# Twenty gathered and twenty-nine multiplied blocks in the first layer of a four-layer graph network, with one-hots of 784 columns

## The chip, the cores and the metric

The kernel runs on one core of one Trainium2 chip. The metric is the time of one execution in microseconds of device time. Three runs of the kernel before took 2024.36, 2024.81 and 2026.46 us; the median is 2024.81 us.

## What is computed

6250 nodes with 256 features each, 100,000 directed edges sorted by destination. The input is normalised and cut at zero, then four layers follow. Each adds to every node the rows of its neighbours (`segment_sum`) and sends the sum through three matrices. Cut to what matters:

```python
def agg(h):
    return jax.ops.segment_sum(h[src], dst, num_segments=N)

for l in range(NL - 1):                     # three layers
    h = x + agg(x)
    h = relu(h @ W1s[l] + b1s[l])
    h = relu(h @ W2s[l] + b2s[l])
    x = h @ W3s[l] + b3s[l]
h = x + agg(x)                              # the head
h = relu(h @ cW1 + cb1)
h = relu(h @ cW2 + cb2)
return h @ cW3 + cb3

h = maximum(layernorm(x), 0.0)
x = x + gnn(h, src, dst, ...)
```

## The kernel before

**Blocks.** The nodes form 49 blocks of 128. The first 24 blocks are re-sorted by degree; they are called "s", and block 0 has the nodes with fewest edges. The other 25 are called "u" and keep their order. The first matrix of a layer is multiplied in ahead of the sum over neighbours, so what a layer adds up is `XY`: for each of the 49 source blocks a high and a low part of 256 columns, kept on chip.

**Two ways to add up.** The sum for a destination block is made in one of two ways.

- *Multiplied.* A block of the adjacency matrix, 49 x 128 x 128 counts of one byte, is built once, stored (`mats`), fetched in each layer (`at<-mat`, line 1279), cast to a number type of the matmul (`a<-at`, lines 1896 to 1901, on ScalarE and VectorE) and multiplied with `XY` on TensorE (line 1928). Destination blocks are taken together in *panels* of up to four. A panel goes through 49 *units*, one for each source block, and a unit has four matmuls of 128 columns for each destination block of the panel.
- *Gathered.* For each node of a degree-sorted block its neighbours' rows are fetched by indirect DMAs that GpSimd issues (`rows<-table`, line 1613), one DMA for each rank of neighbour, and added two at a time: the first pair is copied on ScalarE (line 1645), the others are added on VectorE (lines 1649 and 1651). The sum `u` (lines 1666 and 1667) is transposed on TensorE (`pt`, line 1676).

The lists in `sorted_edges` divide the blocks. `seq` names the 32 blocks that are built, in the order of building; `early`, `wide` and `final` cut them into the panels of layer 0, of layers 1 and 2 and of the head, in places of `seq`; `nodes_of` names the gathered groups of each layer. Before, layer 0 multiplies 30 blocks in panels of 3, 4, 4, 4, 4, 4, 4 and 3, and gathers 19.

**Building.** While layer 0 runs, `build` makes the adjacency blocks, 8 *batches* of 4 one-hot pairs for each block (257 batches in all). A batch is a one-hot `lo` of 4 x 128 columns (line 1197), a one-hot `hi` of 4 x 98 columns times a weight (line 1215, one instruction for each of the four), four matmuls of 98 columns (line 1245) and an eviction to bytes (`at<-bp`, line 1253, every eighth on VectorE at line 1255). The values that are compared with come from small copies on ScalarE (`pairs`, `marks`, lines 1190 and 1192).

**The order of work.** The instruction stream of each engine is fixed when the program is made. `build` and `listed` are generators: one yield of `build` is a batch. `listed` makes the list of the neighbours of the degree-sorted blocks: six groups of three VectorE operations (lines 1702, 1706 and 1711), then the edge lists fetched by GpSimd (`lane<-padded`, line 1734), then six groups that turn them into row numbers (`some`, `idxN`, lines 1752 to 1757), then the rows of the high s blocks for the builder. First comes a stage of `PRE` batches, in which nothing is multiplied yet: 8 for each block of the first panel, and 4 more. Then the panels run, and `goals` spreads the remaining batches over their units, so that a panel's blocks are ready when it begins. In each unit `listed` is taken on by one yield.

The gathers are spread over a layer by a planned clock (`work_of`, `pace`), and each waits for the matmul that was the last one in the program when it was issued, so GpSimd can't run ahead of TensorE by more than planned. `XY` has to be replaced between layers. The MLP of each panel and each gathered group (`second`, line 1408; `third`, lines 1505 and 1510) is put into the units of later panels; its rows go to the next table, s blocks through one indirect DMA each (`place_rows`, lines 594 and 596, a *place*), also on GpSimd, in between the gathers. The last panel of a layer, and the last gathered block, are done in a hurry ahead of the next layer.

Of the kernel before, what the change touches and what calls it, by code (L numbers as in the profile page):

```python
# [9 lines left out]
F32 = mybir.dt.float32  # L10
# [410 lines left out]
def sorted_edges(  # L421
# [39 lines left out]
    nc = tc.nc  # L461
    N, C = x.shape
    (E,) = src.shape
    NLAYER = W1s.shape[0]
# [3 lines left out]
    NT = -(-N // P)  # L468
# [3 lines left out]
    GSUB = 64 // GD  # L472
    TWO = GD // 2
    HW = NT * TWO
# [4 lines left out]
    BATCH = 4  # L479
# [52 lines left out]
    clT = const.tile([P, 3, GSUB, 2 * BUILT], BF16, name="clT")  # L532
# [10 lines left out]
    cT, weigh, loT = clT[:, 0], clT[:, 1], clT[:, 2]  # L543
# [553 lines left out]
    with tc.manual_schedule():  # L1097
# [77 lines left out]

        pairs, marks = {}, {}

        def pair(hots, k):

            if k < len(batches):  # L1180
                slot, s, half, q0 = batches[k]
                if s is None:
                    pairs[slot, 2] = hots.tile([P, BATCH, 2], BF16, name="more", bufs=1)
                    nc.vector.tensor_copy(pairs[slot, 2],
                                          extra[:, 2, :, None].to_broadcast([P, BATCH, 2]))
                    marks[slot, 2] = hots.tile([P, 2, BATCH], F32, name="moremarks", bufs=1)
                    nc.vector.tensor_copy(marks[slot, 2], extra[:, :2])
                elif q0 == 0:
                    pairs[slot, half] = hots.tile([P, GSUB, 2], BF16, name="pairs", bufs=3)
                    nc.scalar.copy(pairs[slot, half], loT[:, :, s, None].to_broadcast([P, GSUB, 2]))  # L1190
# [3 lines left out]
        def one_hot(o, values, which, n):  # L1194

            shape = [P, BATCH, n // 2, 2]
            nc.vector.tensor_tensor(  # L1197
                o.rearrange("p q (n t) -> p q n t", t=2),
                values.rearrange("p (n t) -> p n t", t=2)[:, None, :, :].to_broadcast(shape),
                which[:, :, None, :].to_broadcast(shape), OP.is_equal)  # L1200

        def low_hot(hots, k):
            if k < len(batches):
                slot, s, half, q0 = batches[k]
                lo = hots.tile([P, BATCH, P], BF16, name="lo", bufs=2)
                one_hot(lo, lanes, pairs[slot, 2] if s is None else pairs[slot, half][:, q0:q0 + BATCH], P)
                hot[k] = [lo]

        def high_hot(hots, k):
            if k < len(batches):  # L1210
                slot, s, half, q0 = batches[k]
                hi = hots.tile([P, BATCH, HW], BF16, name="hi", bufs=2)
                w, o = (marks[slot, 2], 0) if s is None else (marks[slot, half], q0)
                for q in range(BATCH):
                    nc.vector.tensor_scalar(hi[:, q, :], cols, w[:, 0, o + q:o + q + 1],  # L1215
                                            w[:, 1, o + q:o + q + 1], op0=OP.is_equal, op1=OP.mult)
                hot[k].append(hi)

        own_at = [None]

        def build(hots, ats, ps_b):


            each = GSUB // BATCH
            pair(hots, 0)
            low_hot(hots, 0)
            high_hot(hots, 0)
            step, held = 0, None
            for k, (slot, s, half, q0) in enumerate(batches):
# [13 lines left out]
                for m in range(BATCH):  # L1243
                    for i, (lo, hi) in enumerate(sets):
                        mm = nc.tensor.matmul(bp[:, m * HW:(m + 1) * HW], lo[:, m, :], hi[:, m, :],  # L1245
                                              start=(i == 0), stop=(i == len(sets) - 1))
# [16 lines left out]
                if s is None:  # L1263
                    held = None
                    low_hot(hots, k + 1)
                    high_hot(hots, k + 1)
                yield
# [429 lines left out]
        def listed(pool, ps_b):  # L1697
# [50 lines left out]
            for b0, n in nodes_of[0]:  # L1748
                r, o = wide_of[b0], starts_of[b0]
                shape = [P, n, r]  # L1750
                some = pool.tile(shape, F32, name="some", bufs=1)
                nc.vector.tensor_tensor(some, colf[:, None, :r].to_broadcast(shape),
# [313 lines left out]
```

## Time and profile before

| | |
|---|---|
| median of three runs | 2024.81 us |
| profiled execution, its own time | 2030.06 us |
| its span, first to last instruction | 2028.2 us |
| TensorE (PE) busy in the span | 1909.6 us, 94% |
| VectorE (DVE) busy | 1118.4 us, 55% |
| ScalarE (ACT) busy | 1080.1 us, 53% |
| GpSimd (POOL) busy | 1304.6 us, 64% |
| mean granted TensorE clock | 0.972 |
| DMA traffic | 361.47 MB, mean 178 GB/s |

The shares are means over stages that differ. The span has a preparation up to about 135 us, the stage of `PRE` batches up to 183.4 us, layer 0 up to 717.6 us, layers 1 and 2 up to 1594 us, and the head. Of the views of the profile, the one by windows gives each engine's busy time in each of these, and the timeline tells what a single instruction waited for. A duration in the timeline is that of the instruction; where one engine's instructions overlap, the distance from start to start tells its rate.

### The profile page before, as it was taken

To read this page: it belongs to the slowest core of one execution; us is meant where nothing else is said; L and a number is where in the kernel's file an instruction comes from. 1 tells how busy PE (TensorE), PEld (TensorE's weight loads), DVE (VectorE), ACT (ScalarE), POOL (GpSimd) and SP (SyncE) were. 2 spreads that over 40 slices of the span, in tenths; PEclk is the share of its full clock that TensorE was granted. 3 is DMA by queue.
4 is the path that set the end of the run, shared out by engine and by line. 5 is a ranking of instruction groups with operands and counts; after the bars stand their busy time and mean duration, and the time that the engine had idled before them with its cause. 6 is when DMAs were issued, how large, how long until landed. Compare 5 with 4: busy or idle time off the path is not lost. (4 is left out here: it accounts for less than half of the span.)

```text
span 2028.2 us, 29980 instructions
## 1 busy us (share of the span) xinstructions
PE 1909.6 (94%) x9236; PEld 1477.3 (73%) x9236; DVE 1118.4 (55%) x2984; ACT 1080.1 (53%) x2228; POOL 1304.6 (64%) x1444
## 2 busy tenths in 40 slices
PE   5856999999999899999999999999999999999997
PEld 3643667677777777777789777777789777777765
DVE  7779989898876634334344443333335344443433
ACT  4634667676676555444444564444445464454442
POOL 2525556666766637677777656776777466777775
PEclk9876999999999999999999999999999999999998
DMA  5513546666656746556556675555557576665553
GB/s 167 172 59 121 166 148 210 198 203 188 208 175 192 227 151 191 171 180 184 170 174 189 195 225 172 169 169 179 179 173 214 160 233 191 197 190 178 181 174 106
DMA packets 252342, 361.47 MB, mean 178 GB/s; under 512 B 33353, under 2 KB 206313, under 8 KB 252155
## 3 DMA queue, kind: packets, MB, share of 16 engines
q1 hardware_dynamic: 188160, 190.34, 29.7%
q0 software_dynamic: 61952, 166.87, 27.6%
q10 hardware_dynamic: 2058, 2.25, 0.4%
q8 instruction: 74, 1.21, 0.3%
q14 instruction: 98, 0.79, 0.1%
HBM read 292.33 MB, written 67.40 MB: 177 GB/s over the span
## 5 line engine op out<-in xcount | busy, mean ns | idle before, releaser
L1928 PE MATMUL agg<-a,XY 128*128 128x512 f32 (+1 forms) x6272 | 1510.7, 393 | 16.0 <-DVE a L1901 9.6
L1613 POOL DMA_INDIRECT rows<-table,idxN x1121 | 1084.0, 967 | 493.5 <-PE agg L1928 205.8
L1928 PEld LDWEIGHTS agg<-a,XY 128*128 128x128 f32 x6272 | 1144.3, 189 | 254.6 <-issue 15.0
L1899 ACT CAST a<-at 128x512 fp32r<-128x512 uint8 (+1 forms) x1249 | 707.4, 601 | 239.6 <-PE agg L1928 228.9
L1649 DVE TENSOR_TENSOR sums<-sums,rows 128x512 f32<-128x512 f32 x477 | 333.1, 698 | 483.9 <-DMA rows<-table,idxN 441.7
L1215 DVE TENSOR_SCALAR hi<-cols,marks 128x98 bf16<-128x98 bf16 x1024 | 250.7, 326 | 0.0
L1901 DVE CAST a<-at 128x512 fp32r<-128x512 uint8 (+1 forms) x312 | 141.2, 459 | 167.4 <-PE agg L1928 141.9
L1253 ACT CAST at<-bp 128x392 uint16<-128x392 f32 x227 | 111.0, 489 | 144.6 <-PE bp L1245 141.6
L1245 PE MATMUL bp<-hi,lo 128*128 128x98 bf16 x1028 | 118.7, 215 | 34.9 <-DVE hi L1215 31.5
L1245 PEld LDWEIGHTS <-lo 128*128 128x128 bf16 x1028 | 61.3, 100 | 111.1 <-DVE hi L1215 65.7
L1408 PE MATMUL ps<-h,w 128*128 128x512 f32 (+2 forms) x336 | 135.8, 548 | 0.0
L1505 PE MATMUL ps<-w,h 128*128 128x256 f32 x588 | 133.7, 379 | 0.0
L1197 DVE TENSOR_TENSOR lo<-lanes,pairs 128x512 bf16<-128x512 bf16 x256 | 107.0, 418 | 29.7 <-PE bp L1245 25.1
L1505 PEld LDWEIGHTS ps<-w,h 128*128 128x128 f32 x588 | 111.2, 190 | 15.8
L596 POOL DMA_INDIRECT table<-zz,ids x72 | 72.1, 1002 | 68.8 <-DVE zz L1510 48.4
L1645 ACT COPY sums<-rows 128x512 f32<-128x512 f32 x74 | 43.8, 592 | 123.8 <-DMA rows<-table,idxN 93.7
L1411 ACT ACTIVATE h<-ps,bias 128x512 f32<-128x512 f32 (+2 forms) x84 | 51.7, 636 | 96.0 <-PE ps L1408 95.8
L1510 DVE TENSOR_TENSOR zz<-ps,w 128x512 f32<-128x512 f32 (+1 forms) x81 | 50.4, 637 | 94.5 <-PE ps L1505 87.5
L1408 PEld LDWEIGHTS ps<-h,w 128*128 128x128 f32 x336 | 63.1, 193 | 52.4 <-issue 37.3
L1684 ACT ACTIVATE h<-pt,bias 128x256 f32<-128x256 f32 (+1 forms) x84 | 33.1, 446 | 126.6 <-PE pt L1676 125.3
L1335 DVE TENSOR_TENSOR XY<-back,XY 128x256 fp32r<-128x256 f32 x138 | 54.1, 421 | 42.5 <-ACT XY L1334 41.9
L1942 ACT ACTIVATE h<-agg,bias 128x512 f32<-128x512 f32 (+1 forms) x60 | 37.3, 670 | 73.5 <-PE agg L1928 73.3
(235 smaller groups left out, 889.3 us busy)
## 6 DMA issues: line engine op xcount, KB each, us to landing
at<-mat SPq DMA_DIRECT2D x140, 448.0 KB
mat<-at SPq DMA_DIRECT2D x32, 784.0 KB
at<-mat SPq DMA_DIRECT2D x62, 336.0 KB
rows<-table,idxN POOLq DMA_INDIRECT x1121
back<-table SPq DMA_DIRECT2D x138, 128.0 KB
table<-zz SPq DMA_DIRECT2D x35, 256.0 KB
at<-mat SPq DMA_DIRECT2D x63, 112.0 KB
own<-zz SPq DMA_DIRECT2D x55, 128.0 KB
```

What stands on the lines that cost most here:

```text
L596: got = nc.gpsimd.indirect_dma_start(out=ap, out_offset=bass.IndirectOffsetOnAxis(ap=ids[:, b:b + 1], axis=0), in_=sb, in_offset=None)
L1197: nc.vector.tensor_tensor(o.rearrange("p q (n t) -> p q n t", t=2), values.rearrange("p (n t) -> p n t", t=2)[:, None, :, :].to_broadcast( ...
L1215: nc.vector.tensor_scalar(hi[:, q, :], cols, w[:, 0, o + q:o + q + 1], w[:, 1, o + q:o + q + 1], op0=OP.is_equal, op1=OP.mult)
L1245: mm = nc.tensor.matmul(bp[:, m * HW:(m + 1) * HW], lo[:, m, :], hi[:, m, :], start=(i == 0), stop=(i == len(sets) - 1))
L1253: nc.scalar.copy(o, v)
L1408: mm = nc.tensor.matmul(ps[:, :w], weights[l][0][:, c, i * P:(i + 1) * P], h1[:, c, :w], start=(c == 0), stop=(c == KC - 1))
L1505: mm = nc.tensor.matmul(o, h2[0][:, c, nodes], w3[:, c, :], start=(c == 0), stop=(c == KC - 1))
L1613: got = nc.gpsimd.indirect_dma_start(out=t[:, c % 2, :], out_offset=None, in_=tables[self.l][:, :], in_offset=bass.IndirectOffsetOnAxis(ap ...
L1649: nc.vector.tensor_tensor(sums, sums, rows.rearrange("p h c -> p (h c)"), OP.add)
L1899: nc.scalar.copy(o, v)
L1901: nc.vector.tensor_copy(o, v)
L1928: mm = nc.tensor.matmul(agg[c][:, :w], XY[:, j, o:o + P], a[:, :w], start=(i == 0 and half == 0), stop=(i == NT - 1 and half == 1))
```

## The change

Layer 0 gathers 20 blocks instead of 19 and multiplies 29 instead of 30, in panels of 2, 3 and six of 4 blocks. `seq` still has 32 blocks, in another order; layers 1 and 2 still multiply 30 blocks, in panels of 4, 4, 4, 4, 3, 4, 4 and 3; the head's panels keep their sizes. `hi` is made for two batches at a time, by one comparison over 8 x 98 columns and one multiplication in place with the weights, and its values come from one copy on ScalarE instead of two.

```diff
-    seq = [("u", b) for b in range(NS, NT - 3)] + [("s", b) for b in range(NS - 1, NS - 6, -1)] + [
-        ("u", b) for b in range(NT - 3, NT)] + [("s", NS - 6), ("s", NS - 7)]
-    early = [(0, 3)] + [(b, 4) for b in range(3, 27, 4)] + [(27, 3)]
-    wide = [(b, 4) for b in range(0, 24, 4)] + [(24, 3), (27, 3)]
+    seq = [("u", b) for b in range(NS, NT - 6)] + [("s", b) for b in range(NS - 1, NS - 5, -1)] + [
+        ("u", b) for b in range(NT - 6, NT)] + [("s", b) for b in range(NS - 5, NS - 8, -1)]
+    early = [(0, 2), (2, 3)] + [(b, 4) for b in range(5, 29, 4)]
+    wide = [(b, 4) for b in range(0, 16, 4)] + [(16, 3), (19, 4), (26, 4), (23, 3)]
...
-    nodes_of = [[(15, 4), (11, 4), (7, 4), (4, 3), (1, 3), (0, 1)]] * NLAYER + [
+    nodes_of = [[(16, 4), (12, 4), (8, 4), (4, 4), (1, 3), (0, 1)]] + [
+        [(15, 4), (11, 4), (7, 4), (4, 3), (1, 3), (0, 1)]] * (NLAYER - 1) + [
         [(13, 4), (9, 4), (5, 4), (1, 4), (0, 1)]]
...
-                    pairs[slot, half] = hots.tile([P, GSUB, 2], BF16, name="pairs", bufs=3)
-                    nc.scalar.copy(pairs[slot, half], loT[:, :, s, None].to_broadcast([P, GSUB, 2]))
-                    marks[slot, half] = hots.tile([P, 2, GSUB], F32, name="marks", bufs=3)
-                    nc.scalar.copy(marks[slot, half], clT[:, :2, :, s])
+                    pairs[slot, half] = hots.tile([P, 3, GSUB, 2], BF16, name="pairs", bufs=3)
+                    nc.scalar.copy(pairs[slot, half],
+                                   clT[:, :, :, s, None].to_broadcast([P, 3, GSUB, 2]))
...
+        def compare(o, values, which, op):
+
+            n, width = o.shape[1], o.shape[2]
+            shape = [P, n, width // 2, 2]
+            o = o.rearrange("p q (n t) -> p q n t", t=2)
+            if values is None:
+                values = o
+            else:
+                values = values.rearrange("p (n t) -> p n t", t=2)[:, None, :, :].to_broadcast(shape)
+            nc.vector.tensor_tensor(o, values, which[:, :, None, :].to_broadcast(shape), op)
...
         def high_hot(hots, k):
             if k < len(batches):
-                slot, s, half, q0 = batches[k]
-                hi = hots.tile([P, BATCH, HW], BF16, name="hi", bufs=2)
-                w, o = (marks[slot, 2], 0) if s is None else (marks[slot, half], q0)
-                for q in range(BATCH):
-                    nc.vector.tensor_scalar(hi[:, q, :], cols, w[:, 0, o + q:o + q + 1],
-                                            w[:, 1, o + q:o + q + 1], op0=OP.is_equal, op1=OP.mult)
-                hot[k].append(hi)
+                codes, o, n = of(k)
+                hi = hots.tile([P, 2 * BATCH, HW], BF16, name="hi", bufs=2)
+                compare(hi[:, :n], cols, codes[:, 0, o:o + n], OP.is_equal)
+                compare(hi[:, :n], None, codes[:, 1, o:o + n], OP.mult)
+                for i in range(n // BATCH):
+                    hot[k + i] = [hi[:, i * BATCH:(i + 1) * BATCH]]
...
                 if s is not None:
                     low_hot(hots, k + 1)
-                    high_hot(hots, k + 1)
+                    if q0 % (2 * BATCH) == 0:
+                        high_hot(hots, k + 2)
...
-                some = pool.tile(shape, F32, name="some", bufs=1)
+                some = pool.tile(shape, F32, name="moved", bufs=2)
```

`lo` is made as before, by `compare` too (it now has line 1201, as the two instructions of `hi` have). The first panel has two blocks, so `PRE` is 8 x 2 + 4 = 20 batches instead of 28.

Three places show how the instructions move. The first is VectorE at the start of the stage of `PRE` batches; `hi` and `lo` are the one-hots, `cols` and `lanes` the column numbers they are compared with, `lane` the first piece of `listed`. Before:

```order
L1053 COPY zs<-bp 128x256
L1197 TENSOR_TENSOR lo<-lanes,pairs 128x512
L1215 TENSOR_SCALAR hi<-cols,marks 128x98 x4
L1197 TENSOR_TENSOR lo<-lanes,pairs 128x512
L1215 TENSOR_SCALAR hi<-cols,marks 128x98 x4
L1702 TENSOR_TENSOR lane<-lanes,goal 128x512
```

and now:

```order
L1054 COPY zs<-bp 128x256
L1201 TENSOR_TENSOR hi<-cols,pairs 128x784
L1201 TENSOR_TENSOR hi<-hi,pairs 128x784
L1201 TENSOR_TENSOR lo<-lanes,pairs 128x512 x2
L1201 TENSOR_TENSOR hi<-cols,pairs 128x784
L1201 TENSOR_TENSOR hi<-hi,pairs 128x784
L1712 TENSOR_TENSOR lane<-lanes,goal 128x512
```

Two batches take ten instructions before and four now, and `hi` stands two batches ahead of the matmuls that read it instead of one.

The second place is TensorE at the end of layer 0's last panel: `agg` are the products, four to a unit, `pt` the transposes of a gathered sum, and `ps` at line 1515 the third matrix of the gathered group of blocks 4 to 7. Before:

```order
L1928 MATMUL agg<-a,XY 128x384 x32
L1676 MATMUL pt<-ident,u 128x128 x2
L1928 MATMUL agg<-a,XY 128x384 x36
L1676 MATMUL pt<-ident,u 128x128 x2
L1408 MATMUL ps<-h_8787,w_1366 128x384 x4
L1928 MATMUL agg<-a,XY 128x384 x4
```

and now:

```order
L1938 MATMUL agg<-a,XY 128x512 x36
L1515 MATMUL ps<-w_1368,h_7852 128x256 x8
L1938 MATMUL agg<-a,XY 128x512 x24
L1686 MATMUL pt<-ident,u 128x128 x2
L1938 MATMUL agg<-a,XY 128x512 x8
L1686 MATMUL pt<-ident,u 128x128 x2
L1938 MATMUL agg<-a,XY 128x512 x4
```

The last row of transposes, at unit 48 of 49 in both, is that of the last gathered block; the third matrix of a gathered group now stands 8 units ahead of it.

The third is GpSimd over the same stretch; `rows` are gathers, `table` with `ids` are places. Before:

```order
L1613 DMA rows<-table_87,idxN 128x256 x5
L596 DMA table_88<-zz,ids 6378x256
L594 MEMSET mark 1x4
...
L596 DMA table_88<-zz,ids 6378x256
L1613 DMA rows<-table_87,idxN 128x256 x5
L1613 DMA rows<-table_87,ids 128x256
```

and now:

```order
L1623 DMA rows<-table_87,idxN 128x256 x9
L597 DMA table_88<-zz,ids 6378x256
L595 MEMSET mark 1x4
...
L597 DMA table_88<-zz,ids 6378x256
L1623 DMA rows<-table_87,idxN 128x256
L1623 DMA rows<-table_87,ids 128x256
```

Four places stand in each; six gathers follow them before, and two now. Over the whole layer the gathers are 330 instead of 309, and the places 20 in both.

More of the change, by code (lines that the diff above doesn't have):

```diff
@@ L1174, in sorted_edges @@
         hot = {}
-        pairs, marks = {}, {}
+        pairs = {}
         def pair(hots, k):
@@ L1194, in one_hot @@
[L1194 to L1200, printed above, removed]
+                    pairs[slot, 2] = hots.tile([P, 3, BATCH, 2], BF16, name="more", bufs=1)
+                    nc.vector.tensor_copy(pairs[slot, 2], extra[:, :, :, None].to_broadcast(
+                        [P, 3, BATCH, 2]))
+                elif q0 == 0:
+                    pairs[slot, half] = hots.tile([P, 3, GSUB, 2], BF16, name="pairs", bufs=3)
+                    nc.scalar.copy(pairs[slot, half],
+                                   clT[:, :, :, s, None].to_broadcast([P, 3, GSUB, 2]))
@@ new lines, in compare, with of @@
+        def compare(o, values, which, op):
[7 more added lines that the diff above has]
+            nc.vector.tensor_tensor(o, values, which[:, :, None, :].to_broadcast(shape), op)
+        def of(k):
+            slot, s, half, q0 = batches[k]
+            if s is None:
+                return pairs[slot, 2], 0, BATCH
+            assert q0 % (2 * BATCH) == 0
+            return pairs[slot, half], q0, 2 * BATCH
@@ L1205, in low_hot @@
                 lo = hots.tile([P, BATCH, P], BF16, name="lo", bufs=2)
[L1206 to L1207 removed]
+                codes, o = (pairs[slot, 2], 0) if s is None else (pairs[slot, half], q0)
+                compare(lo, lanes, codes[:, 2, o:o + BATCH], OP.is_equal)
+                hot[k].append(lo)
         def high_hot(hots, k):
             if k < len(batches):
[L1211 to L1217 removed]
+                codes, o, n = of(k)
[4 more added lines that the diff above has]
+                    hot[k + i] = [hi[:, i * BATCH:(i + 1) * BATCH]]
         own_at = [None]
@@ L1225, in build @@
             pair(hots, 0)
+            high_hot(hots, 0)
             low_hot(hots, 0)
-            high_hot(hots, 0)
             step, held = 0, None
@@ L1243, in build @@
                 for m in range(BATCH):
-                    for i, (lo, hi) in enumerate(sets):
+                    for i, (hi, lo) in enumerate(sets):
                         mm = nc.tensor.matmul(bp[:, m * HW:(m + 1) * HW], lo[:, m, :], hi[:, m, :],
@@ L1264, in build @@
                     held = None
+                    high_hot(hots, k + 1)
                     low_hot(hots, k + 1)
-                    high_hot(hots, k + 1)
                 yield
```

5 lines of the change are left out of this document (removed).

## The prediction

> **What bounds the kernel now.** I read the windows first, cut at the stages of the program: the stage of `PRE` batches, layer 0's first and second panel, its next five, the last but one and the last (the cuts lie within a microsecond of the panels' ends).
>
> ```profile
> core 0: us, PE busy (x) PEld busy (x) DVE busy (x) ACT busy (x) POOL busy (x), PEclk, DMA share, GB/s
> 131.00:183.40 52.40, 27.60 (x140) 12.49 (x139) 48.80 (x182) 18.25 (x52) 16.15 (x18) 0.55 0.26 83
> 183.40:251.00 67.60, 59.31 (x356) 45.62 (x356) 64.00 (x252) 40.11 (x105) 40.15 (x42) 0.92 0.51 158
> 251.00:321.00 70.00, 66.84 (x475) 46.61 (x476) 62.85 (x261) 46.47 (x102) 38.60 (x40) 1.00 0.54 170
> 321.00:585.00 264.00, 263.12 (x1460) 188.28 (x1459) 229.71 (x766) 187.86 (x409) 173.01 (x183) 1.00 0.63 197
> 653.00:718.90 65.90, 54.36 (x292) 46.06 (x293) 35.51 (x97) 38.31 (x97) 37.72 (x41) 0.92 0.58 182
> ```
>
> The first two rows belong to VectorE: 48.80 of 52.40 and 64.00 of 67.60 us busy, while TensorE idles or runs at a low granted clock. From 321 us TensorE is full, and 263.12 of 264.00 us leave only its own work to save. The last row has idle TensorE again. The timeline says what VectorE repeats in the first stage, one batch every 1.25 us:
>
> ```profile
> 135.28 0.42 DVE L1197 TENSOR_TENSOR lo<-lanes,pairs 128x512 bf16<-128x512 bf16 x1 [3.01 <-ACT pairs L1190]
> 137.68 0.68 DVE L1702 TENSOR_TENSOR lane<-lanes,goal 128x512 bf16<-128x512 bf16 x1
> 139.25 0.42 DVE L1197 TENSOR_TENSOR lo<-lanes,pairs 128x512 bf16<-128x512 bf16 x1
> 171.26 0.41 DVE L1197 TENSOR_TENSOR lo<-lanes,pairs 128x512 bf16<-128x512 bf16 x1
> 171.59 1.00 DVE L1215 TENSOR_SCALAR hi<-cols,marks 128x98 bf16<-128x98 bf16 x4
> 171.95 0.93 PE L1245 MATMUL bp<-hi,lo 128*128 128x98 bf16 x4 [0.32 <-DVE hi L1215]
> 172.51 0.41 DVE L1197 TENSOR_TENSOR lo<-lanes,pairs 128x512 bf16<-128x512 bf16 x1
> 183.41 1.62 PE L1928 MATMUL agg<-a,XY 128*128 128x384 f32 x4 [1.99 <-DVE a L1897]
> ```
>
> `lo` takes 0.33 us from start to start, the four `hi` 0.92, and the matmuls wait for `hi`. The last panel's idle time is one wait:
>
> ```profile
> 695.44 1.01 POOL L596 DMA_INDIRECT table<-zz,ids  x1 [0.30 <-issue]
> 696.75 0.99 POOL L596 DMA_INDIRECT table<-zz,ids  x1 [0.21 <-issue]
> 705.68 0.95 POOL L1613 DMA_INDIRECT rows<-table,idxN  x1 [0.30 <-issue]
> 706.93 0.95 POOL L1613 DMA_INDIRECT rows<-table,ids  x1 [0.30 <-issue]
> 711.09 0.69 PE L1676 MATMUL pt<-ident,u 128*128 128x128 f32 x2 [8.69 <-DVE u L1667]
> ```
>
> The last gathered sum is 8.69 us late, because GpSimd works through its queue at 1.25 us a gather and 1.30 us a place, waiting for nothing ("issue").
>
> **The price of a one-hot.** Eight `hi` cost 1.84 us now. The trace has no operation of 784 columns, but two of 512 that bound it. `lane` takes 0.68 us and `lo` 0.41 for as many elements of the same type; they differ in what is broadcast: `lo` reads its values in pairs side by side. So `lo` saves 256 steps of 1.05 ns, two elements a step. The new `hi` has the pairs of `lo`: 0.41 + 136 x 1.05 = 0.55 us long, 0.47 from start to start, and two make 0.94 for two batches. A batch then costs 0.33 + 0.47 = 0.80 us. If the pairs don't help (98 columns are no power of two, and the multiplication is in place), each takes 0.68 + 272 x 1.05 = 0.97, 0.89 from start to start, and a batch is 1.22 us, as today. I take 0.80, since `lo` has the same form, and keep 1.22 as the other end. The Trainium skill ("VectorE: DVE Perf Modes", the side-by-side of a 2048-element operation) speaks against the change: an operation with one tensor may do four elements a cycle, one with two at most two, after about 158 cycles of start. By it the wide pair costs 2 x (158 + 392) / 0.96 = 1.15 us and a batch 0.90, and my sum would come out 8 us longer; `lo`, 0.33 us from start to start where the page gives 0.43, shows that part of the start is hidden, so the trace decides.
>
> **Stage of `PRE` batches.** It lasts 48.1 us (135.28 to 183.41): 28 batches at 1.25 or a little less, about 34, then 9.4 for `listed` (from `lane` to the next `lo` 1.57, six times) and small things. Twenty batches at 0.80 are 16; the rest stays. **Minus 18.5**, products from about 165; with 1.22 it would be minus 10.
>
> **First panel.** Now VectorE-bound. The order gives it 31 batches instead of 39. They cost 25, six groups of row numbers 5 (0.83 each, below), evictions, casts and small operations 6, gather additions some 5: 41 us. TensorE needs less: a block of a panel is the difference of these two windows, products alone, four blocks wide and three:
>
> ```profile
> 389.90:452.00 62.10, 54.34 (x196) 34.24 (x196) 1.00 0.67 209
> 1000.60:1057.50 56.90, 48.06 (x199) 36.73 (x198) 1.00 0.56 169
> 1057.30:1105.00 47.70, 36.51 (x198) 34.20 (x197) 1.00 0.64 195
> ```
>
> That is 11.5 us a block, so two are 25 at most, and 33 batches stretch products by 6.3 and take some time of their own: 0.26 us each, 8 for 31. To the 41 I add a hold. GpSimd fetches the edge lists first:
>
> ```profile
> 165.63 0.98 POOL L1734 DMA_INDIRECT lane<-padded,at  x1 [31.29 <-DVE hi L1215]
> 175.01 0.23 DVE L1752 TENSOR_TENSOR some<-colf,got 128x80 f32<-128x80 f32 x1
> 175.84 0.41 DVE L1197 TENSOR_TENSOR lo<-lanes,pairs 128x512 bf16<-128x512 bf16 x1
> 189.48 0.95 POOL L1613 DMA_INDIRECT rows<-table,idxN  x1 [0.30 <-PE bp L1245]
> 196.26 0.59 ACT L1645 COPY sums<-rows 128x512 f32<-128x512 f32 x1 [2.98 <-DMA rows<-table,idxN]
> ```
>
> The fetches start once `listed` has had some fifteen batches, now about 158, and 20 of them at 1.25 end at 183. So the first gather comes 6 us earlier, the rest of the program 18, and the ScalarE copy that waits for it at 196.26 (2.98 us) will wait longer; casts and evictions queue behind it. I take 4 us (0 to 9): 45 instead of 67.6, **minus 22.5**.
>
> **Second panel.** Three blocks instead of four: minus 11.5. One MLP block less in it (six blocks' worth of these rows is 2 x 2.75, so 1.8 each): minus 1.8.
>
> ```profile
> 1147.92 2.74 PE L1408 MATMUL ps<-h,w 128*128 128x384 f32 x8
> 1157.77 2.75 PE L1505 MATMUL ps<-w,h 128*128 128x256 f32 x12
> L1215 DVE TENSOR_SCALAR hi<-cols,marks 128x98 bf16<-128x98 bf16 x130 | 31.7, 330 | 0.0
> L1649 DVE TENSOR_TENSOR sums<-sums,rows 128x512 f32<-128x512 f32 x17 | 12.2, 720 | 0.1
> ```
>
> (The two rows of a block's MLP are for three blocks.) VectorE falls from 62.85 to about 50 there: 32 batches are 26, gather additions 12, the rest 12. TensorE with 53 us of work decides: **minus 13**.
>
> **Six panels after them.** One is four wide instead of three, plus 11.5; the batches that left the two stages ahead come here, 174 for 158, plus 4; one transpose more, 0.4. The wait at the end stays: from the third matrix at unit 40 to the last transpose lie two additions (1.2), four places (5.2), a gather (1.25) and the way from the last gather to the transpose (706.93 to 711.09, 4.2), 11.8 us, against 8 units and a transpose, 8.2. So 3.6 us if GpSimd keeps up and 8.7 as before if not; I take 8. **Plus 15.**
>
> **The sum.** -18.5 - 22.5 - 13 + 15 = -39. Later: the hurried MLP after layer 0 has four blocks instead of three, +1.8; layers 1 and 2 have one place in their last panel for three, so of the 3.1 us for which layer 1's last transpose waits (second row)
>
> ```profile
> 180.73 1.45 SPq L1279 DMA_DIRECT2D at<-mat  x3
> 1155.19 0.44 PE L1676 MATMUL pt<-ident,u 128*128 128x128 f32 x2 [3.14 <-DVE u L1663]
> ```
>
> about 2.5 go, over both layers; the head gets one place more late, +1.3. More but smaller `at` fetches are hidden, as in layer 0's unaligned panels where TensorE was full; uncovered, each would cost its 0.48 us of issue (1.45 for three, first row). Nearly -39 in all: the span 2028.2 becomes 1989. It belongs to an execution of 2030.06 us; the median of the runs, 2024.81, is 3.4 below the span, so **1986 us**.
>
> **Rivals.** *One-hots no cheaper* (1.22 a batch): stage +8.5, first panel +13, second +9: -9 in all, 2016 us. For it: 784 isn't a power of two, and in place is nowhere shown; against it: `lo`.
>
> *Gathers set the end.* 330 gathers and 20 places at 1.25 and 1.30 are 438 us, from 183 to 622 at the earliest; with the 10.7 from the last gather to the end of the layer (706.93 to 717.6) 632, against 678 by my sum. Before, 412 of 517 us were needed, and most of the difference were waits for TensorE, the planned pace:
>
> ```profile
> POOL rows L1613 <- PE agg L1928: 49.0, 78, 2.1
> POOL rows L1613 <- PE bp L1245: 47.8, 82, 2.2
> DVE sums L1649 <- DMA rows<-table,idxN: 25.2, 11, 6.5
> ```
>
> So gathers alone don't bind; if waits that aren't pace reach 65 us (today below 20) the layer ends near 697: 2005 us.
>
> *Late rows hold the in-order engines: slower.* With 90% of GpSimd's time taken instead of 80, VectorE's additions (25.2 us of waits today) and ScalarE's copies stand in front of one-hots, evictions and casts; TensorE slows, and it paces the gathers. It decides once these waits grow by more than 39 us; at +50 it is 2036 us. Against it: VectorE gets free, so buffers of rows do too.
>
> **Chances.** The forecast 0.72, with its own range 1972 to 2000: down 9 if the first panel comes near TensorE's 36 us and 4 if the end wait is 3.6; up for the hold and the skill's price. One-hots no cheaper 0.09, gathers at the end 0.10, slower 0.07, no change 0.02. A measurement of this kernel can tell 0.2%, 4 us, from no change. Faster 0.90, the same 0.02, slower 0.08. Range 1968 to 2016: the forecast's with the two milder rivals.
>
> **What would show it.** `hi` near 0.55 us and batches 0.80 apart ahead of the first product; first product near 165, second panel from 210, TensorE full from there; layer 0 over near 678 with 4 to 9 us of wait before the last transpose. Wrong would be: `hi` near 0.97; ScalarE's first copy or VectorE's additions waiting many us for rows; a hole over 12 us at the end of layer 0; layers 1 to 3 changed by more than 4 us.

## The result, and the profile after

The changed kernel takes 2010.65 us (median of six runs, 2008.44 to 2013.74), the kernel before 2025.45 us beside it (2022.87 to 2026.86): a ratio of 0.9929, 95% interval 0.9916 to 0.9942, 14.8 us less. The direction was forecast, and the time lies in the range, but the gain is 0.38 of the 39 us that the sum gave. The profiled executions are 20.4 us apart (spans 2028.2 and 2007.8); the account below is theirs. Of the kernel before, the profiled one was 4.6 us above its median. In the changed kernel's rows the line numbers are about ten higher than in those of the kernel before (products 1938 instead of 1928, transposes 1686 instead of 1676, `second` 1418 instead of 1408), and one more or less in the variants below.

The windows of the changed kernel, cut at the same stages as before: the stage of `PRE` batches, layer 0's first and second panel, its next five, its last up to layer 1's first unit, and layer 1's last panel.

```profile
core 0: us, PE busy (x) PEld busy (x) DVE busy (x) ACT busy (x) POOL busy (x), PEclk, DMA share, GB/s
131.00:163.70 32.70, 12.33 (x105) 8.39 (x105) 29.22 (x71) 11.21 (x31) 4.86 (x5) 0.56 0.24 85
163.70:219.40 55.70, 41.73 (x323) 38.37 (x323) 40.96 (x117) 30.34 (x88) 40.74 (x42) 0.80 0.47 144
219.40:275.10 55.70, 52.92 (x473) 44.22 (x473) 49.84 (x161) 39.03 (x94) 37.94 (x38) 0.97 0.61 190
275.10:605.50 330.40, 326.25 (x1826) 235.67 (x1826) 240.64 (x500) 231.47 (x473) 243.13 (x253) 1.00 0.66 205
605.50:686.80 81.30, 70.27 (x326) 51.24 (x326) 43.43 (x91) 46.70 (x103) 54.07 (x59) 0.94 0.65 206
1070.00:1131.50 61.50, 52.48 (x258) 45.53 (x257) 29.11 (x62) 30.60 (x75) 39.10 (x44) 0.97 0.60 186
```

In the first panel VectorE is busy for 40.96 of 55.70 us, so it no longer bounds it by its work, and TensorE is busy for 41.73 of them, at a granted clock of 0.80 (0.92 in this panel before). From there TensorE is nearly full up to the layer's last panel, where 11 us are idle, most of them in one wait:

```profile
679.07 0.66 PE L1686 MATMUL pt<-ident,u 128*128 128x128 f32 x2 [8.64 <-DVE u L1677]
```

Stage by stage, from first unit to first unit:

| stage | before | after | difference | forecast |
|---|---|---|---|---|
| first product at | 183.4 | 163.7 | -19.7 | -18.5 |
| first panel | 67.9 | 55.7 | -12.2 | -22.5 |
| second panel | 70.1 | 55.7 | -14.4 | -13 |
| the other six, to layer 1's first unit | 397.5 | 411.7 | +14.2 | +15 |
| layer 1 | 438.0 | 444.7 | +6.7 | layers 1 and 2 together |
| layer 2 | 437.5 | 441.5 | +4.0 | -0.7 |
| head | 433.8 | 434.8 | +1.0 | +1.3 |

Two rows carry the miss: the first panel (10.3 us) and layers 1 and 2 (11.4 us). They are from single executions: the experiments below show layer 0 to vary by some 3 us between executions with the same streams on TensorE.

**The first panel.** The timeline of the changed kernel: start, duration, engine, line, and in brackets the idle time before and what ended it.

```profile
178.56 0.94 POOL L1744 DMA_INDIRECT lane<-padded,at  x1 [0.30 <-issue]
179.12 0.28 DVE L1765 SCALAR_TENSOR_TENSOR moved<-lane,spot,moved 128x64 f32<-128x64 int32 x1 [2.96 <-DMA lane<-padded,at]
180.08 0.51 PE L1255 MATMUL bp<-hi,lo 128*128 128x98 bf16 x4 [3.35 <-DVE lo L1201]
185.34 0.94 POOL L1744 DMA_INDIRECT lane<-padded,at  x1 [0.31 <-issue]
186.59 0.95 POOL L1623 DMA_INDIRECT rows<-table,idxN  x1 [0.30 <-DMA lane<-padded,at]
192.73 0.59 ACT L1655 COPY sums<-rows 128x512 f32<-128x512 f32 x1 [7.79 <-DMA rows<-table,idxN]
193.70 1.22 PE L1938 MATMUL agg<-a,XY 128*128 128x256 f32 x4 [5.56 <-ACT a L1909]
194.16 0.61 DVE L1201 TENSOR_TENSOR hi<-cols,pairs 128x784 bf16<-128x784 bf16 x1 [4.11 <-ACT pairs L1189]
```

VectorE reaches the row numbers of a group before its edge lists are there and stands for 2.96 us; TensorE misses its one-hot for 3.35. GpSimd gets to the first gather only at 186.59, after twenty fetches: 2.9 us earlier than before, where the first product comes 19.7 us earlier. ScalarE has long come to the copy of the first rows and stands for 7.79 us; the casts and the `pairs` behind it keep TensorE waiting for 5.56 us and VectorE for 4.11.

**Layers 1 and 2.** GpSimd's first and last gather of layer 1 in the kernel before (its last transposes and the second matrices ahead of them, 1155.19 and 1147.92, stand in the prediction):

```profile
745.14 1.15 POOL L1613 DMA_INDIRECT rows<-table,idxN  x1 [10.62 <-ACT a L1899]
1150.66 0.95 POOL L1613 DMA_INDIRECT rows<-table,idxN  x1 [0.30 <-PE ps L1408]
```

and in the changed kernel, with what follows the last gather:

```profile
716.43 1.09 POOL L1623 DMA_INDIRECT rows<-table,idxN  x1 [13.06 <-ACT a L1909]
1118.37 0.94 POOL L1623 DMA_INDIRECT rows<-table,idxN  x1 [0.30 <-issue]
1124.56 0.42 DVE L1673 TENSOR_TENSOR u<-u,sums 128x256 f32<-128x256 f32 x1
1125.03 0.69 PE L1686 MATMUL pt<-ident,u 128*128 128x128 f32 x2 [4.79 <-DVE u L1673]
1125.51 4.04 PE L1418 MATMUL ps<-h,w 128*128 128x384 f32 x8
```

From first to last gather the layer takes 405.5 us before and 401.9 after; 290 gathers at 1.25 and the 20 places behind the first gather (19 after) at 1.30 are 388 of that. GpSimd is all but full, so a layer ends when its last gather is followed by what must come behind it: 6.2 us up to layer 2's first unit (1156.9) before, 13.1 us (1131.5) after. Counted from the layer's first unit, the first gather comes 3.4 us later (29.6 us instead of 26.2), which the shorter stretch of gathers makes up; so these 6.9 us are what layer 1 lost. Of them 2.1 lie between the last gather and the last transposes (6.7 us instead of 4.5), for a reason not followed here, and 4.8 behind the transposes. Those come with the order on TensorE. Before, the second matrices (`second`) of the last gathered group but one stand ahead of the last transposes and fill the wait for them. Now they stand behind: TensorE waits 4.79 us, and then they take 4.04 us instead of 2.74. In the program they were at unit 45 with the transposes at 47; now both are at unit 46 in layer 1 and at 48 in layer 2, transposes first.

### The profile page after: what moved, and what is told of

Read it like the earlier page. It is cut to its first block, busy times and chain, and to the rows that moved or that the text cites. A ratio compares the mean times of both kernels' runs of the same rounds, so it can differ in the third digit from the quotient of the medians.

```text
span 2007.8 us, 29137 instructions
## 1 busy us (share of the span) xinstructions
PE 1877.7 (94%) x9238; PEld 1472.3 (73%) x9238; DVE 1039.6 (52%) x2221; ACT 1066.2 (53%) x2160; POOL 1332.0 (66%) x1468
## 4 chain that ended last, share of the span: by engine, by line
PE 78%; DVE 7%; DMA 7%; issue 3%; POOL 2%; ACT 2%; SPq 0%; DVEq 0%; ACTq 0%; POOLq 0%
PE agg L1938 61%; PE ps L1418 6%; PE ps L1515 6%; DMA rows<-table,idxN 5%; PE bp L1255 2%; PE bp L1047 1%; POOL lane L1744 1%; PE pt L1686 1%; DVE sums L1659 1%; POOL rows L1623 1%; DVE hi L1201 1%; DVE lo L1201 1%; DMA back<-table 1%; PE ps L1432 1%; DVE ws L769 0%
## 5 line engine op out<-in xcount | busy, mean ns | idle before, releaser
L1938 PE MATMUL agg<-a,XY 128*128 128x512 f32 (+2 forms) x6272 | 1500.3, 391 | 21.8 <-ACT a L1909 9.7
L1623 POOL DMA_INDIRECT rows<-table,idxN x1141 | 1108.3, 971 | 444.9 <-PE agg L1938 167.9
L1909 ACT CAST a<-at 128x512 fp32r<-128x512 uint8 (+2 forms) x1249 | 704.1, 598 | 242.9 <-PE agg L1938 233.6
L1659 DVE TENSOR_TENSOR sums<-sums,rows 128x512 f32<-128x512 f32 x486 | 338.3, 696 | 485.0 <-DMA rows<-table,idxN 424.0
L1418 PE MATMUL ps<-h,w 128*128 128x512 f32 (+3 forms) x336 | 138.4, 556 | 1.8 <-DVE zz L1520 1.8
L1255 PE MATMUL bp<-hi,lo 128*128 128x98 bf16 x1028 | 95.4, 219 | 31.7 <-DVE lo L1201 31.1
L1421 ACT ACTIVATE h<-ps,bias 128x512 f32<-128x512 f32 (+3 forms) x84 | 51.4, 636 | 85.4 <-PE ps L1418 85.4
L1952 ACT ACTIVATE h<-agg,bias 128x512 f32<-128x512 f32 (+2 forms) x60 | 37.0, 667 | 73.5 <-PE agg L1938 68.2
L1201 DVE TENSOR_TENSOR hi<-cols,pairs 128x784 bf16<-128x784 bf16 x128 | 71.9, 562 | 7.2 <-ACT pairs L1189 7.2
L1201 DVE TENSOR_TENSOR hi<-hi,pairs 128x784 bf16<-128x784 bf16 x128 | 72.7, 568 | 4.4
```

The source lines that it names most:

```text
L1201: nc.vector.tensor_tensor(o, values, which[:, :, None, :].to_broadcast(shape), op)
L1418: mm = nc.tensor.matmul(ps[:, :w], weights[l][0][:, c, i * P:(i + 1) * P], h1[:, c, :w], start=(c == 0), stop=(c == KC - 1))
L1421: later(soon, lambda: nc.scalar.activation(h2[0][:, i, :w], ps[:, :w], AF.Relu, bias=b2[l][:, i:i + 1]))
L1623: got = nc.gpsimd.indirect_dma_start(out=t[:, c % 2, :], out_offset=None, in_=tables[self.l][:, :], in_offset=bass.IndirectOffsetOnAxis(ap ...
L1659: nc.vector.tensor_tensor(sums, sums, rows.rearrange("p h c -> p (h c)"), OP.add)
L1909: nc.scalar.copy(o, v)
```

## The experiments

The theory after this has three parts: the one-hots bring the gain; the first panel loses part of it to lists and first rows that come too late; and the new order of layers 1 and 2 gives some 10 us back by the place of eight matmuls. The rivals are that layers 1 and 2 suffer from the panel of four at the end of layer 0 (a longer hurried MLP, later gathers) or from their own panels, that the first panel is bound by something else, and that the twentieth block carries the gain.

**The one-hots alone.** The changed kernel with the four table statements of the kernel before:

```diff
-    early = [(0, 2), (2, 3)] + [(b, 4) for b in range(5, 29, 4)]
+    early = [(0, 3)] + [(b, 4) for b in range(3, 27, 4)] + [(27, 3)]
...
(seq, wide and nodes_of likewise as before)
```

> The kernel before with the new one-hots alone: 19 blocks gathered, 30 multiplied, the old panels and the old order of layers 1 and 2. If the price of the one-hots carries the change: the stage of 28 batches shortens by 28 x 0.45 = 12.6 us (first product near 171), the first panel by 13 to 15 (VectorE has 39 x 0.45 = 17.5 us less work there, minus a hold), the second by up to 3, and layers 1 to 3 are as before: 25 to 30 us less than the kernel before, so FASTER than the changed kernel by 10 to 15. Rival, the twentieth gathered block carries a good part: 8 to 14 us less than the kernel before, slower than the changed kernel.

Ratio 0.9907 (0.9891 to 0.9923), 19 us less than before: less than the forecast of 25 to 30, but at least as much as the whole change. Its windows:

```profile
131.00:175.90 44.90, 17.82 (x146) 12.10 (x145) 38.79 (x96) 17.62 (x45) 13.64 (x13) 0.54 0.27 92
175.90:239.20 63.30, 52.50 (x357) 43.54 (x357) 50.98 (x136) 39.33 (x94) 43.61 (x45) 0.86 0.56 169
```

The first product comes 7.5 us earlier instead of 12.6, and the first panel is 4.6 us shorter instead of 13 to 15, though VectorE is busy for only 50.98 us of it: TensorE stands once for 5.94 us there, for an eviction behind ScalarE's first copy of rows:

```profile
192.12 0.59 ACT L1654 COPY sums<-rows 128x512 f32<-128x512 f32 x1 [7.80 <-DMA rows<-table,idxN]
193.58 0.49 PE L1254 MATMUL bp<-hi,lo 128*128 128x98 bf16 x4 [5.94 <-ACT at L1262]
```

So late rows take part of the gain with the old tables too. Layer 1 begins at 697.5 us: 21.4 of the 32.1 us that the changed kernel gained up to there. The tables gained the other 10.7. In the profiles they lost 8.2 of them later, in layers 1 and 2 and the head; by the ratios of the runs, all of them.

**The order of layers 1 and 2 alone.** The kernel before with the new `seq` and `wide`:

```diff
-    wide = [(b, 4) for b in range(0, 24, 4)] + [(24, 3), (27, 3)]
+    wide = [(b, 4) for b in range(0, 16, 4)] + [(16, 3), (19, 4), (26, 4), (23, 3)]
...
(and seq as in the change)
```

> The kernel before with the new order of blocks (seq) and the new panels of layers 1 and 2 alone; one-hots, gathered blocks and layer 0's panels as before. Theory, the new order costs the end of layers 1 and 2, because the second matrices of the last group but one stand behind the last transposes on TensorE: each of the two layers 3 to 5 us longer, 6 to 10 us slower in all, the wait before their last transposes over 4 us. Rival, layers 1 and 2 got longer because layer 0 ends with a panel of four (its hurried MLP, gathers that begin later): within 2 us of the kernel before.

Ratio 1.0045 (1.0032 to 1.0058), 9 us slower. Layer 1 takes 444.7 us and layer 2 443.3 (438.0 and 437.5 before): 6.7 and 5.8 us longer, more than the 3 to 5 expected, although layer 0 here ends with its old panel of three. The waits before their last transposes are 4.76 and 3.31 us, the second below the 4 expected. The rival of the longer hurried MLP falls.

**The place of the second matrices alone, in the kernel before.** One number: the step of the last group but one may come three units later.

```diff
-                              last=now[0] + wait + (0 if hurry else SPAN),
+                              last=now[0] + wait + (0 if hurry else SPAN if far == FAR else SPAN + 3),
```

> The kernel before, where the second matrices of the last group but one may run three units later, so that in layers 1 and 2 they stand behind the last transposes, as in the changed kernel; panels, order of blocks, gathers and layer 0 as before. Theory, this place alone is what layers 1 and 2 lost: each 3 to 4 us longer, 6 to 8 us slower in all. Rival, the panels of layers 1 and 2 cost the time (a panel of four as the last but one) and the place of the matrices doesn't matter: within 2 us of the kernel before.

Ratio 1.0050 (1.0037 to 1.0062), 10 us slower. The end of layer 1:

```profile
1146.28 0.94 POOL L1613 DMA_INDIRECT rows<-table,idxN  x1 [0.30 <-issue]
1150.70 0.69 PE L1676 MATMUL pt<-ident,u 128*128 128x128 f32 x2 [5.12 <-DVE u L1663]
1151.19 5.22 PE L1408 MATMUL ps<-h,w 128*128 128x384 f32 x8
```

Layers 1 and 2 are 3.7 and 3.8 us longer, as expected, with the old panels and the old `seq`; the panels are not needed for this loss. But the new order alone cost these layers 12.5 us in its profile, 5 more than the place of the matrices does here, so the rival of the panels is not out for the rest. The head lost 6.0 us, which the expectation had left out: its last transposes wait for 3.32 us instead of 1.64, with its second matrices behind them. TensorE's stream up to layer 1 is the kernel's before, yet layer 1 begins at 715.2 instead of 718.9: so 3.7 us, as much as one profile's stages may be off by, are chance in layer 0.

**The same place put right in the changed kernel.** The step may come four units earlier, and the last sum of a layer is not called for ahead of its last units:

```diff
-                return now[0] >= ends[self.l] - 2 or clock[0] >= self.first + self.acts[0][0] * self.pace
+                return now[0] >= ends[self.l] - 2 or (
+                    len(self.acts) > 1 and clock[0] >= self.first + self.acts[0][0] * self.pace)
...
-                              last=now[0] + wait + (0 if hurry else SPAN),
+                              last=now[0] + wait + (0 if hurry else SPAN if far == FAR else 2),
```

> The changed kernel; the second matrices of the last group but one may run up to four units earlier, and the last transposes of a layer never before its last unit. In layers 1 and 2 the second matrices then stand ahead of the last transposes, as in the kernel before. Theory, that order is what these layers lost: the waits before their last transposes (4.79 and 4.19 us) shrink to 1.5 or less, each layer 3 to 4 us shorter, 6 to 8 us in all. Rival, the layers got longer because gathers begin later or are slower: the wait stays or moves, less than 2 us in all.

Ratio 0.9861 (0.9846 to 0.9875), 28 us less than before and some 14 less than the changed kernel: more than the 6 to 8 forecast. The end of layer 1:

```profile
1114.59 2.74 PE L1418 MATMUL ps<-h,w 128*128 128x384 f32 x8
1122.53 0.44 PE L1687 MATMUL pt<-ident,u 128*128 128x128 f32 x2 [0.98 <-DVE u L1674]
1122.81 2.75 PE L1515 MATMUL ps<-w,h 128*128 128x256 f32 x12
```

The wait is 0.98 us, and the eight matmuls take 2.74 again. In the profiles layer 1 wins 2.9 us, layer 2 5.3 (its first gather also comes 18.8 us after its first unit instead of 24.2, probably since the third matrices moved up too), the head 0.9. So layers 1 and 2 get 8.2 of their 10.7 us back; layer 1 stays 3.8 us longer than in the kernel before, and what that is was not isolated. 2.5 more are gained up to layer 1, in layer 0's first panel (52.8 us instead of 55.7), in which the streams of TensorE, VectorE and ScalarE are the same in both kernels: chance again.

**Row numbers six units later.** For the first panel, one number in `listed`; the fetches stay where they are.

```diff
-            for _ in range(7):
+            for _ in range(13):
```

> The changed kernel with the row numbers of the first group worked out six units later (and with them the first copy of gathered rows); the edge lists are fetched when they were. Theory, the first panel loses its time to VectorE's wait for edge lists and ScalarE's wait for the first rows: the waits of 3.35 and 5.56 us on TensorE go, the first panel is 47 to 50 us instead of 55.3, and the time falls by 5 to 8 us. Rival, the panel is bound by VectorE's own work or by rows that stay late: first panel 53 or more, the time within 2 us of the changed kernel.

Ratio 0.9901 (0.9887 to 0.9915), by the ratios 6 us less than the changed kernel, and its interval only just clears that of the changed kernel. The first and the last panel of layer 0 in its windows:

```profile
164.70:212.90 48.20, 38.52 (x322) 34.76 (x322) 39.53 (x115) 30.61 (x88) 36.93 (x38) 0.87 0.52 155
600.30:684.60 84.30, 72.07 (x326) 52.04 (x327) 43.40 (x92) 47.12 (x103) 55.00 (x60) 0.92 0.64 201
```

The first panel falls to 48.2 us and the wait for lists is gone, but 4.64 us of wait on the first rows are left, since ScalarE still stands for 5.47 us:

```profile
190.94 0.59 ACT L1655 COPY sums<-rows 128x512 f32<-128x512 f32 x1 [5.47 <-DMA rows<-table,idxN]
192.30 0.48 PE L1255 MATMUL bp<-hi,lo 128*128 128x98 bf16 x4 [4.64 <-ACT at L1263]
```

Single profiles vary, so all that have this panel are worth comparing: without the edit it lasts 55.7, 52.8 and 52.7 us (the changed kernel and two variants), with it 48.2, 49.3, 49.9 and 49.8 us (this run and three variants below). The edit is worth 4.4 us on the mean, 2.8 at the least. And layer 1 begins only 2.2 us earlier than in the changed kernel: the last panel has become 3 us longer, with 8.40 us of wait before its last transposes. Most of what the first panel gained was given back at the layer's end. The profiled execution, the slowest of its five, is no shorter than that of the changed kernel (spans 2008.7 and 2007.8), so the 6 us of the runs are not seen in its stages.

**Panels of two and seven fours, 19 gathered.** The one-hots alone, with one more statement changed:

```diff
-    early = [(0, 3)] + [(b, 4) for b in range(3, 27, 4)] + [(27, 3)]
+    early = [(0, 2)] + [(b, 4) for b in range(2, 30, 4)]
```

> The kernel with the new one-hots, 19 blocks gathered, the order of blocks and panels of layers 1 and 2 of before; layer 0 in panels of two and seven of four. Theory, a narrower first panel gains what the first product comes earlier: first product near 164, layer 0 over 7 to 10 us earlier than with the one-hots alone (697.5 us there), so that the twentieth gathered block is worth only 1 to 4 us of layer 0 (686.8 us in the changed kernel). Rival, the gain is the twentieth block's products: layer 0 ends within 3 us of 697.5.

Layer 1 begins at 690.7 us: 6.8 earlier than with the one-hots alone, just under the 7 to 10 expected, and the twentieth block is worth the remaining 3.9. Yet the whole takes 0.9949 (0.9935 to 0.9962), about 8 us more than the one-hots alone; in the profiles it is 1.7 us more (spans 2012.1 and 2010.4). Layer 1's first gather comes 33.9 us after the layer's first unit instead of 26.5; so in absolute time it stands where it stood (724.7 and 724.0), and the 6.8 us were gone by then. A last panel of four may leave more of the MLP to be done first, but that was not tested, and with the same last panel the first gather comes after 29.6 us in the changed kernel and after 22.4 in its best variant below. What layer 0 hands on is here the first gather of layer 1, not TensorE's first unit.

**Both edits, and layer 0's plan.** First the two edits above, later row numbers and second matrices ahead, both in the changed kernel; then, besides, layer 0's gathers planned to end 12 us earlier:

```diff
-                self.pace = (begun[self.l] + work_of(self.l) - CLOSE - self.first) / len(self.order)
+                self.pace = (begun[self.l] + work_of(self.l) - (CLOSE if self.l else 14.0) - self.first) / len(self.order)
```

> The changed kernel with the row numbers six units later and the second matrices ahead of the last transposes, both. If the two places are independent, the sum of the two gains: ratio to the kernel before near 0.983, 5 to 6 us below the one with the second matrices alone. If a shorter first panel is given back at layer 0's end, where GpSimd is late, no more than 2 us below it.

> The same, and layer 0's gathers planned to end 12 us earlier. Theory, the wait of 8.4 to 8.6 us before layer 0's last transposes is the planned pace, and GpSimd has room to gather earlier (13 us idle in the last five panels): the wait falls below 3 us and the time by 5 to 8 us more. Rival, GpSimd is full: the wait stays over 6 us, the time within 2 us of the former.

Both edits give 0.9858 (0.9844 to 0.9872), no better than the second matrices alone: the first panel's gain is given back, as the second half of that expectation had it (the wait before layer 0's last transposes is 9.19 us there). With the earlier plan it is 0.9796 (0.9783 to 0.9809), 1986.43 us, 41 us less than before: faster than both kernels, and 11 us or more below the run with both edits, where 5 to 8 were expected. Its timeline at the end of layer 0 and the first gather of layer 1:

```profile
665.91 2.74 PE L1418 MATMUL ps<-h,w 128*128 128x384 f32 x8
668.20 4.14 PE L1939 MATMUL agg<-a,XY 128*128 128x512 f32 x16
672.17 0.38 PE L1687 MATMUL pt<-ident,u 128*128 128x128 f32 x2
698.08 1.08 POOL L1624 DMA_INDIRECT rows<-table,idxN  x1 [12.95 <-ACT a L1910]
```

The last transposes wait for nothing, and the layer's last panel up to layer 1 has no idle TensorE:

```profile
606.50:675.70 69.20, 69.18 (x336) 51.85 (x337) 39.80 (x85) 47.66 (x104) 44.89 (x50) 1.00 0.71 222
```

So the wait of 8.6 us was the planned pace, not a full GpSimd. Layer 1's first gather is at 698.1 instead of 716.4.

**Around that version.** The same edits with the old tables; two of them in the kernel before; all but the later row numbers; and a plan 20 us earlier instead of 12 (`22.0` for `14.0`).

> The new one-hots with the old tables (19 blocks gathered, old panels and order) and the three edits of the former run: row numbers six units later, second matrices ahead of the last transposes, layer 0's gathers planned to end 12 us earlier. Theory, with the layers' ends in order the tables (narrow first panel, twentieth block) are worth the 10.7 us that they gave layer 0: ratio near 0.985, 8 to 12 us above the former run. Rival, the tables are worth nothing: within 3 us of it, ratio near 0.980.

Ratio 0.9823 (0.9810 to 0.9835): 5.5 us above, between the two expectations. With the layers' ends in order the tables are worth about half of what they gave layer 0.

> The kernel before with two of the edits: second matrices ahead of the last transposes, layer 0's gathers planned to end 12 us earlier. Theory, the wait of 8.7 us at the end of layer 0 was pace in this kernel too: it falls below 2 us and the time by 7 to 12 us. Rival, in this kernel places and gathers at the end fill GpSimd: under 3 us.

Ratio 0.9953 (0.9941 to 0.9965), some 9.5 us less than before. No wait of TensorE in layer 0's last panel is longer than 0.31 us: there too the wait was pace.

> The former run (all the edits) without the later row numbers. Theory, the shorter first panel was given back only because GpSimd's plan decided layer 0's end; with gathers earlier it counts: 3 to 6 us slower than with all. Rival, gathers still decide: within 2 us of it.

Ratio 0.9853 (0.9839 to 0.9868): 10 to 12 us slower than with the later row numbers, by medians and by ratios, more than the 3 to 6 expected. The profiled executions are 5.1 apart (spans 1991.2 and 1986.1; the former was the fastest of its four). Of these, 2.0 come ahead of the first product, where the two kernels do not differ, and 3.9 are in layer 0, 2.8 of them in its first panel. Now the first panel's time counts; the profiles do not show where the rest of the 10 us is.

> All the edits, with layer 0's gathers planned to end 20 us earlier instead of 12. If GpSimd still has room, the first gather of layer 1 and with it the rest come 2 to 5 us earlier. If GpSimd is full by then: within 2 us of the run with 12.

Ratio 0.9843 (0.9830 to 0.9855): 9 us worse, which neither expectation had. In the profile 5 us of it are in layer 0's last panel (74.2 us instead of 69.2 up to layer 1's first unit, 3.9 of them idle), 2.0 come ahead of the first product, which the edit doesn't touch, and layer 1's first gather is at 705.1. The cause was not followed further.

## Why the prediction was right and wrong

**The price of a one-hot: right in the main, a little low.** `hi` takes 562 and 568 ns (550 forecast); the rival of one-hots no cheaper is out. From start to start, in the changed kernel's timeline:

```profile
160.16 0.56 DVE L1201 TENSOR_TENSOR hi<-cols,pairs 128x784 bf16<-128x784 bf16 x1
160.75 0.57 DVE L1201 TENSOR_TENSOR hi<-hi,pairs 128x784 bf16<-128x784 bf16 x1
161.24 0.75 DVE L1201 TENSOR_TENSOR lo<-lanes,pairs 128x512 bf16<-128x512 bf16 x2
161.91 0.57 DVE L1201 TENSOR_TENSOR hi<-cols,pairs 128x784 bf16<-128x784 bf16 x1
```

Two batches take 161.91 - 160.16 = 1.75 us, so a batch is 0.875, not 0.80: the multiplication starts 0.59 us after the comparison that it reads, not 0.47. The estimate from the Trainium skill ("VectorE: DVE Perf Modes", the side-by-side of a 2048-element operation), 0.90, was the nearer one.

**The stage of `PRE` batches, the second panel, the other six, the head: right in size**, -19.7 for -18.5, -14.4 for -13, +14.2 for +15, +1.0 for +1.3; of the 3.7 us of chance in the profiled kernel before, 2.9 lie in the six and would make them +17. Some of this is luck. In the stage of `PRE` batches the dearer batch costs 1.5 us more than the sum had; but the stage began 1.5 us earlier (first one-hot at 133.8 instead of 135.3), and what was taken to stay in it shrank by about as much. A difference of 1 us in the head is within chance. The end wait of 8 was measured as 8.64, but for another reason than the one given: it is the plan, and not the places and gathers that GpSimd has to get through.

**The first panel: wrong in one term.** "I add a hold ... I take 4 us (0 to 9)." VectorE's work there was forecast as 41 us and measured as 40.96; the hold is 14.7, since the panel lasts 55.7 (and 11.7 or more in the two other profiles with this panel). The prediction saw that the first gather comes 6 us earlier and the rest of the program 18, and still took 4 of these 12 us, for ScalarE's copy alone; as measured, the first gather came only 2.9 us earlier. ScalarE's wait grew from 2.98 to 7.79 us, VectorE got one of 2.96 us for lists that had not been late before, and each counts for what is queued behind it: 3.35 and 5.56 us on TensorE, whose clock fell besides. Row numbers six units later took the wait for lists away and 2.8 us or more off the panel (4.4 on the mean), which shows this wait as one cause. The wait on the first rows stayed, 4.64 us on TensorE there and 5.9 with all edits; that it makes up most of the remaining hold is read from the timelines, as no run took it away.

**Layers 1 and 2: wrong in sign.** "Layers 1 and 2 have one place in their last panel for three, so ... about 2.5 go." They grew by 10.7 us, where the 1.8 of the hurried MLP was forecast to be more than balanced. (Layer 1's first panel did grow by 1.7, but by 2.1 with the new order alone, where the hurried panel is still of three blocks; so the MLP isn't shown as the reason.) The step counted GpSimd's places ahead of the last gather and not what stands on TensorE around the last transposes. That place alone made these two layers 7.5 us longer in the kernel before (and the head 6.0, which the change did not do), the new order alone 12.5, and the edit that undoes the place in the changed kernel won 8.2 there. So the place is shown as the cause of most of the loss; some 3 us of it (5 with the new order alone), which may belong to the panels, stay open.

**The rivals.** That gathers set the end was half right in mechanism: in layers 1 and 2 they do, and in layer 0 their plan does, but not by the lateness that the rival priced. Late lists and rows did hold the in-order engines, for some 9 us of TensorE in the first panel, not for 39. Named as signs of a wrong forecast were ScalarE's first copy waiting many us and layers 1 to 3 changed by more than 4: both came.

## What to carry to other kernels

When one engine's work gets cheaper, go through its stream and that of its neighbours for the first waits on things whose time does not move (here lists and first rows from GpSimd), and price each by what is queued behind it; move the waiting instruction back by the time saved. At the end of a stage that a second engine nearly fills, ask what stands behind the last hand-over on the first: eight matmuls behind two transposes instead of ahead of them cost 10 us here, over two layers and the head. And measure a stage by the event that the next one depends on; time gained at another point may be gone before it.

## What the runs showed of the hardware

In these traces, work behind a long wait on TensorE paid twice. The same eight matmuls take 2.74 us when TensorE has been busy, 4.04 us after an idle time of 4.79 us and two transposes, and 5.22 us after 5.12 us: 1.9 times as long. The granted clock of these stretches (the column behind the five engines) is the reason: 2.74 / 0.67 is 4.09 and 2.74 / 0.52 is 5.27. The rows are from the kernel before, the changed kernel, and the kernel before with the second matrices behind:

```profile
1147.92:1150.60 2.68, 2.68 (x10) 1.62 (x10) 0.00 (x0) 0.58 (x1) 1.92 (x2) 1.00 0.45 136
1125.51:1129.50 3.99, 3.99 (x10) 2.23 (x10) 0.14 (x1) 2.23 (x5) 0.00 (x0) 0.67 0.00 0
1151.19:1156.40 5.21, 5.21 (x10) 2.85 (x10) 0.00 (x0) 0.63 (x2) 0.00 (x0) 0.52 0.00 0
```

The loss does not simply follow the length of the wait: behind the 4.19 us in layer 2 of the changed kernel the eight matmuls take 4.88 us, more than behind 4.79. The Trainium skill ("TensorE: Matmul & The Clock Gate", "Part 1: The HAM clock gate") has the array at half its clock after an idle window of about 3.4 us; these rows agree.
